# First tree of a Winograd factorization-machine kernel: W11 in two halves, P1 ahead of P5, the fifth linear product in another PSUM tile

## The chip, the cores and the metric

The kernel runs on one core of a Trainium2 chip. Its time is the device time of one execution in microseconds; the figure for the kernel before is the median of three runs, 1403.03 us (1402.93 to 1405.4).

## The reference

A layer of a factorization machine on a batch of 1024 rows, all in float32:

```python
# x (1024, 512), weight (64, 512, 512), lin_w (512, 512), lin_b (512,)
out_lin = x @ lin_w.T + lin_b
xv = einsum('bf,efm->bem', x, weight)
zp = einsum('bf,efm->bem', square(x), square(weight))
return out_lin + 0.5 * sum(square(xv) - zp, axis=1)
```

Nearly all the work is `xv`: a product of 1024x512 by 512x32768, whose result is squared and summed over the 64 embeddings.

## The kernel before, in words

**Tiling.** The 32768 columns are cut into 16 groups of 32 outputs by 64 embeddings. In each group the product goes by two levels of the Strassen-Winograd scheme, seven products in place of eight at each level. The outer level has seven "trees" (`tree(s, g, i, order)`, i from 1 to 7); the first group runs them in the order `ORDER_0 = (1, 2, 6, 7, 5, 4, 3)`. Inside a tree there are seven products `P1` to `P7`; each is two `matmul` calls (two blocks of 128 batch rows, 512 columns each), which the profile shows as four MATMUL records of 128x512 each. The operands of X, seven outer ones with seven inner ones each, live in `x_all` and are made once, at the start, by ScalarE's copies and VectorE's sums (DVE in the profile).

**One tree.** For i = 1 the right-hand matrix is the quadrant W11, in the tile `w11` of shape [128, 2, 2, 512]: the first index of two is the column half c, the second the row half k. So `b11, b21` lie in half c = 0 and `b12, b22` in half c = 1. Four differences come first: `t1 = b12 - b11`, `t2 = b22 - t1`, `t3 = b22 - b12`, `t4 = b21 - t2`. P1 takes b11, P2 takes b21, P3 takes b22, P4 to P7 take t4, t1, t2, t3. In the first tree t1 and t2 are made by VectorE, t3 and t4 by GpSimd (POOL).

**PSUM.** A product writes one of four tiles `b1`, `b3`, `b2_0`, `b2_1`, each of 128x1024 float32. P5 goes to `b3`, ScalarE (ACT) copies it to `p5`, P3 is added to `b3`, ScalarE copies that to `p53`. P1 goes to `b1`, ScalarE copies it to the tree's `b2`, and only then may P2 be added to `b1` and P6 to `b2`. After P6 VectorE adds `b2 + p53` into `oa1`, and then P7 may be added to `b2`; after P7 it adds `b2 + p5` into `oa3`, and then P4 may be added.

**Order.** Nothing is ordered by hand except TensorE's (PE's) products: a product of the tree with place s gets the key `7*s + PLACE[p]`, and for the first tree `7*s + PLACE_0[p]`, and PE takes the keys in rising order. Products of neighbouring trees thus alternate. For the other engines, `Plan.order()` plays the plan through with estimated costs and gives every engine a fixed list, the operation that is needed earliest first among those that its model holds ready. On the chip each engine runs its list in order, with semaphores for the waits. So a change of keys or of an estimated landing can reorder the lists of all engines.

**The start.** Before the trees come four products of the linear layer's own Strassen-Winograd scheme (`lin_product`: 1, 2, 4, 5; keys -1000 to -997), while x and the linear weights still arrive. Their transfers are issued by hand at the head of the two DMA queues (`load_x`, `load_lw`: nine and two on SP's queue), and `landing(name, at)` tells the planner when each is expected. Then `load(g, q)` issues the weight quadrants on SP's queue, in the first group in the order W11, W21, W12, W22, each of 1 MB. After its PSUM result a linear product is copied out by two ScalarE operations with bias (`lin_copy`), each of one half of the tile; the fifth one writes `outer7`, which lies in `w22b`.

ScalarE also squares every quadrant for `zp` (`w_squares`: `wsq<-w`, two per quadrant). In ScalarE's list these stand between the copies of PSUM.

The beginning of PE's list before, in the numbering of the products (the prime marks the second tree, i = 2, on W21): linear 1, 2, 4, 5, then P5 (b3), P1 (b1), P3 (b3), P6 (b2), P5' (b3), P2 (b1), P3' (b3), P7 (b2), P1' (b1). ScalarE's list there: two bias copies of linear product 5, `p5<-b3`, `b2<-b1`, first squares of W12, `p53<-b3`, second squares of W12.

Of the kernel before, what the change touches and what calls it, by code (L numbers as in the profile page):

```python
# [23 lines left out]
SLOT = {1: 0, 7: 1, 2: 2, 4: 3, 5: 4, 6: 5, 3: 6}  # L24

PLACE = {5: -6, 3: -2, 1: 0, 6: 3, 2: 4, 7: 6, 4: 9}
PLACE_0 = {**PLACE, 5: -6, 1: -3, 3: -2, 6: -1}
PE, DVE, ACT, POOL, SP = "PE", "DVE", "ACT", "POOL", "SP"
NONE = ""

# [172 lines left out]
def kernel(  # L203
# [39 lines left out]
    nc = tc.nc  # L243
    NG, NQ, _, NCB, KH, N = weight.shape
# [20 lines left out]
    buf = {}  # L265
# [44 lines left out]
    def two_input(engine, o, a, b, sub, size=1024):  # L310

        costs = {DVE: 0.08 + 1.06 * size / 1024, POOL: 0.14 + 2.19 * size / 1024}

        def emit(e):
            f = engines[e].tensor_sub if sub else engines[e].tensor_add
            f(o, a, b)  # L316

        return {engine: costs[engine]}, emit

    def whole(o, a, b, psum=False):  # L320

        costs, emit = two_input(DVE if psum else POOL, buf[o], buf[a], buf[b], False)
        plan.add(costs, emit, (a, b), (o,))
# [21 lines left out]
    def dma(o, i, reads, writes, move=1.75, on=(SP,)):  # L345
        plan.add(dict.fromkeys(on, 0.45), lambda e: queues[e].dma_start(o, i), reads, writes,
                 land=2.0, move=move)
# [4 lines left out]
    def landing(name, at):  # L352
        plan.add({SP: 0.0}, None, (), (name,), land=at - 2 * plan.HOP)

    def load_x(h, k, lo, hi, at):

        n, r = f"oa{2 * h + k // KH}", k % KH
        nc.sync.dma_start(buf[n][:, r, lo * Q:hi * Q], x_src[:, k, h * H + lo * Q:h * H + hi * Q])
        for u in range(lo, hi):
            landing((n, r, u), at)  # L360
# [20 lines left out]
    load_lw(nc.sync, [2, 3], 1, 9.2)  # L381
    for at, k in enumerate((2, 3, 0, 1)):
        load_x(1, k, 0, 2, 10.0 + 0.8 * at)
    nc.scalar.dma_start(bias[:], lin_b)
    landing("bias", 9.5)
    nc.scalar.preload_act_table(AF.Square)
# [62 lines left out]
    def lin_product(p, bank, first, key, last=None, by_k=False):  # L449

        (a, a_names), (b, b_names) = lhs[p], rhs[p]
        for at, key in enumerate((key, last or key + 0.2) + (key + 0.4, key + 0.6) * by_k):
            if by_k:
                k, u = divmod(at, 2)
                steps = [(k, c, slice(u * Q, (u + 1) * Q)) for c in range(2)]
                names = a_names[at:at + 1] + b_names[k:k + 1]
                tiles = both_halves(bank)
            else:
                steps = [(k, at, slice(0, H)) for k in range(KH)]
                names = a_names + b_names  # L460
                tiles = ((bank, at),)

            def emit(_, steps=steps):
                for k, c, rows in steps:
                    nc.tensor.matmul(  # L465
                        buf[bank][:, c, rows], b[:, k, ts(c, P)], a[:, k, rows],
                        start=first and k == 0 and rows.start == 0, stop=k == KH - 1,
                        skip_group_check=True,
                    )

            plan.add({PE: PAIR / (1 + by_k)}, emit, names + tiles, tiles, key=key)

    def both_halves(bank):
        return (bank, 0), (bank, 1)
# [52 lines left out]
    def lin_store(n, h, c):  # L527
        dma(lin_dram[:, ts(c, 2), ts(h, H)], buf[n], (n,), (("lind", h, c),))
# [10 lines left out]
    def lin_copy(n, bank, c, sign):  # L539

        for u in range(2):
            plan.add(
                {ACT: 0.56},
                lambda _, u=u: nc.scalar.activation(
                    buf[n][:, u, :], buf[bank][:, u, :], AF.Identity,
                    bias=bias[:, 2 * c + u:2 * c + u + 1], scale=sign,
                ),
                ((bank, u), "bias"), ((n, u),),
            )
        used(n, (n, 0), (n, 1))  # L550
# [6 lines left out]
    def used(*names):  # L557

        plan.add({NONE: 0.0}, None, (), names)
# [7 lines left out]
    lin_product(4, "b2_0", True, -998)  # L567
    lin_copy("c_2", "b2_0", 0, 1.0)
    lin_store("c_2", 1, 0)
    lin_product(5, "b1", True, -997)  # L570
    flat = buf["w22b"].rearrange("p c k n -> p (c k) n")
    buf["outer7"], buf["negative"] = flat[:, 0::3], flat[:, 1:3]
    used("outer7", ("lt", 1), ("lt", 4))
    lin_copy("outer7", "b1", 1, -1.0)
    lin_store("outer7", 1, 1)
    lin_store("outer7", 0, 1)
    used("quads", *(("ob0", r, c) for r in range(KH) for c in range(2)), ("ob1", 0, 0), ("ob1", 1, 0))
# [19 lines left out]
    def w(g, q):  # L597
        return q + "ab"[g % 2] if q == "w22" else q

    def load(g, q):  # L600
        n = w(g, QUAD[q])
        dma(buf[n], weight[g, q], (), (n,), 3.5)

    def load_more(n, src, reads=(), move=5.5, view=lambda ap: ap):
# [45 lines left out]
    def tree(s, g, i, order):  # L650
        r = w(g, RHS[i])
        b11, b21, b12, b22 = (buf[r][:, c, k, :] for c in range(NCB) for k in range(KH))
        t = {k: t_ring[k]() for k in range(1, 5)}
        for k, a, b, reads in (
            (1, b12, b11, (r,)),
            (2, b22, buf[t[1]], (r, t[1])),
            (3, b22, b12, (r,)),
            (4, b21, buf[t[2]], (r, t[2])),
        ):
            engine = POOL if s or k > 2 else DVE  # L660
            costs, emit = two_input(engine, buf[t[k]], a, b, True, 512)
            plan.add(costs, emit, reads, (t[k],), both=engine == DVE)
        rhs = {
            1: (b11, r), 2: (b21, r), 3: (b22, r), 4: (buf[t[4]], t[4]),
            5: (buf[t[1]], t[1]), 6: (buf[t[2]], t[2]), 7: (buf[t[3]], t[3]),
        }

        def product(p, b, first):
            op, name = rhs[p]

            def emit(_):
                for j in range(G):
                    nc.tensor.matmul(  # L673
                        buf[b][:, j, :], buf[f"X{i}"][:, SLOT[p], ts(j, P)], op,
                        start=first, stop=True, skip_group_check=True,
                    )

            plan.add({PE: PAIR}, emit, (name, f"{'Y' if p == 7 else 'X'}{i}", b), (b,),
                     key=7 * s + (PLACE if s else PLACE_0)[p])

        def copy(o, b):
            act(buf[o], buf[b], None, (b,), (o,))

        def target(pos):
            if i == 2 and order.index(2) < order.index(6):
                return c_ring()
            return f"{TARGET[i]}{pos}"

        def early(pos):

            return pos == 3 and i in ADDEND_FROM and (
                order.index(i) - order.index(ADDEND_FROM[i]) > 1
            )

        def outer_psum(b, pos):

            if i == 1:
                copy(f"oa{pos}", b)
            elif i == 5:
                o = c_ring()  # L700
                whole(o, f"oa{pos}", b, psum=True)
                whole(f"ob{pos}", f"ob{pos}", b, psum=True)
                finish(g, i, o, pos)
            else:
                o = target(pos)
                whole(o, b, f"{ADDEND[i]}{pos}", psum=True)
                if i in (2, 4, 3):
                    finish(g, i, o, pos)

        def outer_sbuf(b, p, pos):  # L710

            if i == 1:
                whole(f"oa{pos}", b, p, psum=True)
            elif i == 5:
                o = c_ring()
                whole(p, b, p, psum=True)
                whole(o, f"oa{pos}", p)
                whole(f"ob{pos}", f"ob{pos}", p)
                finish(g, i, o, pos)
            else:  # L720
                a, o = f"{ADDEND[i]}{pos}", target(pos)
                if early(pos):
                    whole(o, b, p, psum=True)
                else:
                    z = p if o == a else o
                    whole(z, b, p, psum=True)
                    whole(o, z, a)
                if i in (2, 4, 3):
                    finish(g, i, o, pos)

        b2, p5, p53 = b2_ring(), p5_ring(), p53_ring()
        product(5, "b3", True)
        if early(3):
            whole(p5, "b3", f"{ADDEND[i]}3", psum=True)
        else:
            copy(p5, "b3")
        product(3, "b3", False)
        copy(p53, "b3")
        product(1, "b1", True)
        copy(b2, "b1")  # L740
        product(6, b2, False)
        outer_sbuf(b2, p53, 1)
        product(2, "b1", False)
        outer_psum("b1", 0)
        product(7, b2, False)
        outer_sbuf(b2, p5, 3)
        product(4, b2, False)
        outer_psum(b2, 2)
# [184 lines left out]
    for g in range(NG - 1):  # L933
        group(g, {} if g else {2: lin_tree})
        b, names = turn(g, 3)
        m, c = (g * MG) % P, g * MG // P
# [295 lines left out]
```

## Time and profile before

| what | value |
|---|---|
| time, median of three runs | 1403.03 us |
| the profiled execution's own time | 1403.01 us |
| its span (first to last instruction) | 1401.2 us |
| PE busy | 1395.3 us (100%), 3314 records, granted clock 1.00 |
| VectorE, ScalarE, GpSimd busy | 1099.9, 714.9, 1053.3 us |
| landing of W11, W21, W12, W22 of the first group | 17.0, 19.5, 22.0, 24.4 us |
| first product of the first tree starts | 19.26 us |

Times in the trace count from the start of the span. The profiled execution is 1.8 us longer than its span, and 0.02 us from the median. A MATMUL record of 128x512 lasts 592 ns but the next one starts 429 ns after it, so a gap between records only shows in "idle before" when it is longer than the overlap; start times tell more. The landings are the issue times of the transfers plus the time to landing that the view of line L346 gives for each.

### The profile page before, as it was taken

The page shows a single profiled execution, that of the slowest core. Times are in us where ns is not written, and L with a number is a line of the kernel's source. Part 1 is how long each engine was busy: PE and PEld are TensorE (multiplying, and loading weights), DVE is VectorE, ACT ScalarE, POOL GpSimd, SP SyncE. Part 2 cuts the span into 40 slices and gives each one's busy share as a digit, 9 for nine tenths or more (in the row PEclk, how much of TensorE's full clock was granted, in tenths as well). Part 3 has the DMA queues.
Part 4 walks back from the last instruction along what each step waited for, and adds up shares of the span by engine and source line. Part 5 has one row for each costly group of instructions (what it writes and reads, how often), then busy time and mean ns, then how long its engine had stood idle before and what let it go on. Part 6 is the DMA issues. An engine that isn't in the chain of part 4 may idle for free.

```text
span 1401.2 us, 10709 instructions
## 1 busy us (share of the span) xinstructions
PE 1395.3 (100%) x3314; PEld 629.8 (45%) x3314; DVE 1099.9 (78%) x987; ACT 714.9 (51%) x756; POOL 1053.3 (75%) x750
## 2 busy tenths in 40 slices
PE   9999999999999999999999999999999999999998
PEld 4544444444444444444444444444444444444454
DVE  7998696877959788696877959678696877959676
ACT  4555473545736456373544636355373544636444
POOL 4796776958778586786958678686786958678994
PEclk9999999999999999999999999999999999999999
DMA  7495574827749285582817538183572817538363
GB/s 270 94 221 162 138 180 121 226 74 180 205 121 232 90 196 164 135 221 82 225 51 180 153 99 206 49 196 120 132 178 84 222 53 180 154 97 207 101 165 113
DMA packets 55815, 212.90 MB, mean 152 GB/s; under 512 B 21520, under 2 KB 23056, under 8 KB 33872
## 3 DMA queue, kind: packets, MB, share of 16 engines
q0 software_dynamic: 13136, 84.81, 31.5%
q1 hardware_dynamic: 40352, 125.12, 25.6%
q10 hardware_dynamic: 2272, 2.30, 0.5%
q8 instruction: 27, 0.44, 0.1%
q14 instruction: 28, 0.23, 0.0%
HBM read 180.75 MB, written 14.02 MB: 139 GB/s over the span
## 4 chain that ended last, share of the span: by engine, by line
PE 96%; DVE 1%; DMA 1%; ACT 0%; issue 0%; SPq 0%; DVEq 0%
PE b L673 93%; PE b L826 2%; PE b L465 1%; DMA c<-xT 1%; PE b L1145 1%; DMA oa<-xT 0%; DVE p L316 0%; DVE c L316 0%; DVE ob L316 0%; DVE w_sum L339 0%; ACT ob L332 0%; DVE oa L316 0%; DVE acc L339 0%; ACT c L332 0%; ACT b L328 0%
## 5 line engine op out<-in xcount | busy, mean ns | idle before, releaser
L673 PE MATMUL b<-t,x_all 128*128 128x512 f32 x1792 | 806.4, 592 | 0.2 <-DVE oa L316 0.2
L673 PEld LDWEIGHTS b<-t,x_all 128*128 128x128 f32 x1792 | 340.2, 190 | 426.1 <-issue 417.3
L673 PE MATMUL b<-w,x_all 128*128 128x512 f32 x768 | 358.1, 592 | 0.0
L316 POOL TENSOR_TENSOR t<-w 128x512 f32<-128x512 f32 x127 | 171.3, 1349 | 148.5 <-PE b L673 78.1
L328 ACT COPY p<-b 128x1024 f32<-128x1024 f32 x165 | 165.6, 1003 | 171.0 <-PE b L673 166.2
L673 PEld LDWEIGHTS b<-w,x_all 128*128 128x128 f32 x768 | 145.9, 190 | 183.7 <-issue 182.5
L316 POOL TENSOR_TENSOR t<-w,t 128x512 f32<-128x512 f32 x127 | 171.8, 1353 | 55.1 <-PE b L673 54.8
L332 ACT ACTIVATE oa<-oa 128x1024 f32<-128x1024 f32 x124 | 129.5, 1057 | 144.2 <-DVE oa L316 144.2
L328 ACT COPY b<-b 128x1024 f32<-128x1024 f32 (+1 forms) x114 | 113.5, 996 | 135.7 <-PE b L673 132.0
L673 PE MATMUL b<-T,x_all 128*128 128x512 f32 x384 | 180.3, 592 | 0.0
L339 DVE TENSOR_REDUCE acc<-oa 128x16 f32<-128x1024 f32 x124 | 148.8, 1211 | 36.7 <-ACT oa L332 36.7
L339 DVE TENSOR_REDUCE w_sum<-wsq 128x16 f32<-128x1024 f32 x128 | 153.6, 1209 | 0.3 <-ACT wsq L332 0.2
L332 ACT ACTIVATE c<-c 128x1024 f32<-128x1024 f32 x77 | 79.6, 1055 | 131.6 <-DVE c L316 88.2
L316 DVE TENSOR_TENSOR oa<-b,p 128x1024 f32<-128x1024 f32 x95 | 115.7, 1218 | 33.7 <-PE b L673 33.5
L316 POOL TENSOR_TENSOR t<-T 128x512 f32<-128x512 f32 x64 | 85.7, 1339 | 53.2 <-issue 31.3
L673 PEld LDWEIGHTS b<-T,x_all 128*128 128x128 f32 x384 | 73.0, 190 | 91.0 <-issue 89.4
L316 DVE TENSOR_TENSOR p<-b,p 128x1024 f32<-128x1024 f32 x79 | 96.4, 1220 | 20.9 <-PE b L673 16.8
L316 DVE TENSOR_TENSOR ob<-b,p 128x1024 f32<-128x1024 f32 x48 | 58.6, 1221 | 64.7 <-PE b L673 64.4
L332 ACT ACTIVATE wsq<-w 128x1024 f32<-128x1024 f32 x96 | 98.3, 1054 | 12.0 <-DMA w<-weight 11.1
L316 POOL TENSOR_TENSOR t<-T,t 128x512 f32<-128x512 f32 x64 | 82.4, 1288 | 20.1 <-PE b L673 20.0
L316 POOL TENSOR_TENSOR c<-oa,p 128x1024 f32<-128x1024 f32 x32 | 84.8, 2651 | 0.0
L316 DVE TENSOR_TENSOR oa<-b,oa 128x1024 f32<-128x1024 f32 x62 | 75.6, 1220 | 9.5 <-PE b L673 9.5
(116 smaller groups left out, 1421.4 us busy)
## 6 DMA issues: line engine op xcount, KB each, us to landing
w<-weight SPq DMA_DIRECT2D x48, 1024.0 KB, 5.4
T<-weight POOLq DMA_DIRECT2D x45, 1024.0 KB, 9.2
T<-weight SPq DMA_DIRECT2D x30, 1024.0 KB, 7.2
w<-weight POOLq DMA_DIRECT2D x16, 1024.0 KB, 11.0
w<-T POOLq DMA_DIRECT2D x16, 1024.0 KB, 6.9
w22a<-weight SPq DMA_DIRECT2D x8, 1024.0 KB, 10.8
w22b<-weight SPq DMA_DIRECT2D x8, 1024.0 KB, 10.9
c<-xT SPq DMA_DIRECT2D x9, 512.0 KB, 6.8
```

Source lines behind the costliest of these rows:

```text
L316: f(o, a, b)
L328: nc.scalar.copy(o, i)
L332: nc.scalar.activation(o, i, func)
L339: lambda _: nc.vector.tensor_reduce(o, i.rearrange("p a (m e) -> p a m e", e=E), axis=AX.X, op=ALU.add),
L465: nc.tensor.matmul(buf[bank][:, c, rows], b[:, k, ts(c, P)], a[:, k, rows], start=first and k == 0 and rows.start == 0, stop=k == KH - 1, ...
L673: nc.tensor.matmul(buf[b][:, j, :], buf[f"X{i}"][:, SLOT[p], ts(j, P)], op, start=first, stop=True, skip_group_check=True,)
L826: nc.tensor.matmul(buf[b][:, u, lo:lo + Q], op[z], buf[f"X{x}"][:, SLOT[p], :], start=first and not lo, stop=True, skip_group_check=True,)
L1145: nc.tensor.matmul(o, ap[:, k, ts(u, P)], in_rows(o, buf[raw[i]][:, k, lo:hi]), start=first and k == 0, stop=k == 1, skip_group_check=True,)
```

## The change

```diff
-PLACE_0 = {**PLACE, 5: -6, 1: -3, 3: -2, 6: -1}
+PLACE_0 = {**PLACE, 1: -6, 5: -5, 2: -4, 3: -3, 6: -2, 7: 3}
...
     for at, k in enumerate((2, 3, 0, 1)):
         load_x(1, k, 0, 2, 10.0 + 0.8 * at)
+    for c in range(NCB):
+        nc.sync.dma_start(buf["w11"][:, c], weight[0, 0, :, c])
+        landing(("w11", c), 14.5 + 1.5 * c)
...
-    lin_product(5, "b1", True, -997)
+    lin_product(5, "b3", True, -997)
...
-    lin_copy("outer7", "b1", 1, -1.0)
+    lin_copy("outer7", "b3", 1, -1.0)
...
     def load(g, q):
         n = w(g, QUAD[q])
+        if not g and not q:
+            return used(n, (n, 0), (n, 1))
         dma(buf[n], weight[g, q], (), (n,), 3.5)
...
+        own = r if s else (r, 0)
         rhs = {
-            1: (b11, r), 2: (b21, r), 3: (b22, r), 4: (buf[t[4]], t[4]),
+            1: (b11, own), 2: (b21, own), 3: (b22, r), 4: (buf[t[4]], t[4]),
```

Three things change. The transfer of W11 in the first group is issued by hand, as two transfers of 512 KB, and in the first tree P1 and P2 wait for the first half alone. The keys of the first tree put P1 first, then P5, P2, P3, P6, and P7 at key 3. The fifth product of the linear layer goes to `b3` in place of `b1`, so that P1 finds `b1` free.

PE's list after the linear products becomes: P1 (b1), P5 (b3), P2 (b1), P3 (b3), P6 (b2), P5' (b3), P7 (b2), P3' (b3), P1' (b1). ScalarE's list there: two bias copies of linear product 5 (now from `b3`), first squares of W12, `b2<-b1`, `p5<-b3`, second squares of W12, `oa0<-b1`, `p53<-b3`. VectorE's first 24 operations keep their order. GpSimd's first operation is t1 of W21, then t3 of W11; before, it was the other way round. SP's queue has one transfer more; the order of the others stays. Number and kinds of all other instructions are unchanged, and the lists differ in single swaps until about a quarter of the run.

## The prediction

> **What bounds the kernel now.** I read the page's busy line first, then the chain, then PE's own waits.
>
> ```profile
> PE 1395.3 (100%) x3314; PEld 629.8 (45%) x3314; DVE 1099.9 (78%) x987; ACT 714.9 (51%) x756; POOL 1053.3 (75%) x750
> ...
> PE 96%; DVE 1%; DMA 1%; ACT 0%; issue 0%; SPq 0%; DVEq 0%
> ```
>
> PE is busy for 1395.3 of 1401.2 us, at a granted clock of 1.00, and the change adds and removes no product. So the time can only change by the idle time of PE. PE's waits over the whole span:
>
> ```profile
> PE b L465 <- DMA oa<-xT: 1.1, 1, 1.1
> PE b L391 <- PEq L1221: 0.8, 1, 0.8
> PE b L673 <- DVE oa L316: 0.2, 1, 0.2
> ```
>
> The first two end at 7.04 us, in the loads of x, ahead of everything that is touched. The third lies at 461 us, where the lists of all engines are the same again. What is left to gain sits at the start of the first tree, below the threshold of that view, and shows in the start times of PE's timeline:
>
> ```profile
> 15.73 3.60 PE L465 MATMUL b<-x_all,w22b 128*128 128x512 f32 x8
> 19.26 1.98 PE L673 MATMUL b<-t,x_all 128*128 128x512 f32 x4
> 21.08 3.17 PE L673 MATMUL b<-w,x_all 128*128 128x512 f32 x7
> ```
>
> In steady state four records (one product) take 1.72 us and eight 3.43 (the chain has such pieces throughout), and a group of four shows 1.88 to the end of its last record. From 15.73 the next product is due at 19.16, but starts at 19.26, 0.10 late, and lasts 1.98 instead of 1.88: the weight load that could not run ahead. Its cause is VectorE's t1, which starts at 17.45 and takes 1.75, to 19.20. So 0.20 us is all that the first tree loses now: a gain of 0.2% (2.8 us, about what a measurement of this kernel can tell from no change) isn't there to be had. It can only lose. Therefore I follow the new lists of PE and ScalarE through the next twelve microseconds. ScalarE's timeline, and the transfer of W12 in the view of line L346 (window 10.52 to 10.9: issued at 10.54, landed 11.4 later, 21.97 us):
>
> ```profile
> 19.36 1.27 ACT L544 ACTIVATE w22b<-b,bias 128x512 f32<-128x512 f32 x2 [2.17 <-PE b L465]
> 21.28 1.01 ACT L328 COPY p<-b 128x1024 f32<-128x1024 f32 x1 [0.65 <-PE b L673]
> 23.05 1.00 ACT L328 COPY b<-b 128x1024 f32<-128x1024 f32 x1 [0.76 <-PE b L673]
> 23.96 1.06 ACT L332 ACTIVATE wsq<-w 128x1024 f32<-128x1024 f32 x1
> ```
>
> ```profile
> L346 SPq DMA_DIRECT2D w<-weight x1: 430/430/430, 10.5 to 10.5; - x1
> ...
> DMA to landing us min/median/max: 11.4/11.4/11.4
> ```
>
> Now the squares of W12 start two microseconds after its landing, behind both copies.
>
> **The change part by part.**
>
> *P1 first, on W11.* W11 as a whole lands at 17.02 (issue 9.59 plus 7.4), so P1 starts at 19.16 when linear product 5 leaves PE, and the two halves are not needed for that. b1 is free: VectorE's sum that read it ended at 13.79 (VectorE's timeline: 12.57 plus 1.22). P5 follows at 20.88 and has t1, done by 19.20 (earlier, if GpSimd no longer works beside it: 512 columns took 0.68 us at 9.69), and b3, whose two bias copies end at 20.63. Gain 0.20.
>
> *The wait that the change adds.* In ScalarE's new list the first squares of W12 stand ahead of `b2<-b1`. ScalarE is free at 20.63 and waits for W12 until 21.97. Squares 22.00 to 23.06; the next operation starts 0.10 before the end, as the rows above do, so the copy of P1's result runs 22.96 to 23.96. P2 adds to b1, is due at 20.88 + 1.72 = 22.60, and starts at 24.00: 1.40 late, plus the 0.10 of an exposed weight load. Loss 1.50. PE has nothing else in its list, since it too goes in order.
>
> *What is queued behind.* `p5<-b3` runs to 24.87, and P3 is due at 24.00 + 1.82 = 25.82: covered by 0.9. P6 at 27.54 has b2 and t2 (20.26 plus 1.75 on VectorE). P5' at 29.26 needs `p53<-b3`: P3's last record ends at 27.70, the copy at 28.72, covered by 0.5. P7 at 30.97 is the tightest: P6's last record ends at 29.42, VectorE's add (free since 27.85, takes 1.21) at 30.65, covered by 0.3. If that add took 1.75, as such operations do beside GpSimd, it would cost 0.2. t3 of W11 now follows t1 of W21 on GpSimd: 19.56 + 1.90 + at most 1.9 gives 23.4, seven microseconds before P7. I take nothing for these.
>
> *Two transfers for one.* One more issue costs SP 0.47 us (9.59, 10.06, 10.54 are the issues now), so W12 is issued at 11.01, W22 at 11.49. The transfers ahead end at 19.49, so the issue is covered by 8 us. What counts is W12's landing. Nearest rows: 1 MB loads land 2.47 apart (17.02, 19.49, 21.97), and the 512 KB stores `lind` behind them 1.28 apart (25.72, 26.99, 28.27, 29.55, each the issue plus its time to landing). Two halves thus take 2.56 at most where the whole takes 2.47, and I take W12 at 22.0. But W11 itself took 4.32 after the last load of x (issued 9.11, landed 3.6 later), 1.85 over the 2.47, and the trace does not say why. Bounds: the halves remove that 1.85 (W12 at 20.1), or each half pays it (W12 at 23.8).
>
> [...]
>
> *The sum.* -0.20 + 1.50 = +1.30 us. From the span 1401.2 that makes 1402.5; from the median (0.02 over the profiled execution) 1403.03 + 1.30 = 1404.3 us.
>
> **The rivals.**
>
> *The wait vanishes.* If W12 lands at 20.1, ScalarE squares 20.53 to 21.59 and copies to 22.5, just before P2 is due. Then only the gain remains: 1403.03 - 0.20 = 1402.8. For it: the unexplained 1.85 us sit exactly on the transfer that is split. Against it: P2's stall shrinks one for one with the landing only, and the bytes ahead of W12 are the same. Partial cases lie between.
>
> *Slower by over 0.2%.* Same place, other sign: both halves pay the 1.85, W12 lands at 23.8, P2 is 3.35 late with its load, and the time is 1403.03 - 0.20 + 3.35 = 1406.2. It decides from a landing of 23.5 on (1.5 late). Against it: the 512 KB rows above. The tight cover of P7 (0.2) would add to it, and of the three runs before one stood 2.4 us over the median, so a median can fall there too.
>
> *The change does not do what it says.* P1 doesn't need the first half early, since the whole lands 2.1 us before PE is free. This is certain rather than a rival, and already in the sum: the halves bring nothing on the path.
>
> **How the numbers follow.** Forecast (W12 within 0.7 us of 22.0: 1403.6 to 1405.0, reaching to 1405.8 with a small extra wait): 0.68. Wait gone or nearly (1402.8 to 1403.6): 0.12. Slower by over 0.2% (above 1405.8): 0.18. Faster by over 0.2%: 0.02, because PE's idle time in the touched stretch is 0.2 us. That makes faster 0.02, same 0.68 + 0.12 = 0.80, slower 0.18. The range goes from 1402.8, the sum without the wait, to 1406.2, the upper bound of the landing.
>
> **What would show it.** In PE's waits after, one new row: b at the product line, ended by ScalarE's b copy, about 1.4 us, at 24.0 us in the timeline. In ScalarE's timeline: squares of w idle before by 1.3 us until a DMA, at 22.0, then b, then p. PE's first product of the tree at 19.16 with `b<-w,x_all`. The chain should run through ScalarE at this place to the DMA of w. All the rest of PE's rows should be shifted by 1.3 us and still whole at 461. The prediction is wrong if W12 lands before 21 or after 23.5 us, if the copy of b1 does not wait for the squares, or if a stall appears after 30 us.

## The result, and the profile after

The changed kernel takes 1405.76 us (median of 20 runs, 1404.6 to 1408.62), the kernel before 1402.68 (median of 20, 1402.18 to 1405.4). The ratio is 1.0023 with a 95% interval of 1.0016 to 1.003: slower by 3.1 us. The profiled execution took 1406.77, its span is 1405.0, 3.78 over the span before. PE's busy line on the page, and PE's waits over the whole span:

```profile
PE 1397.2 (99%) x3314; PEld 630.3 (45%) x3314; DVE 1093.8 (78%) x987; ACT 714.1 (51%) x756; POOL 1049.6 (75%) x750
```

```profile
PE b L679 <- ACT b L328: 2.2, 1, 2.2
PE b L394 <- PEq L1227: 0.8, 1, 0.8
PE b L468 <- DVE x_all L316: 0.3, 1, 0.3
```

The first row is new, at the line of the products and ended by ScalarE's `b` copy, as forecast. Before, there was no wait of that kind; but it is 2.2 us and not 1.4, and PE is busy for 1.9 us more although it does the same 3314 records. ScalarE's timeline of the changed kernel gives the cause, and the view of line L346 (window 10.2 to 10.3) the landing of W12:

```profile
19.20 1.26 ACT L547 ACTIVATE w22b<-b,bias 128x512 f32<-128x512 f32 x2 [2.76 <-PE b L468]
22.77 1.06 ACT L332 ACTIVATE wsq<-w 128x1024 f32<-128x1024 f32 x1 [2.30 <-DMA w<-weight]
23.73 1.01 ACT L328 COPY b<-b 128x1024 f32<-128x1024 f32 x1
24.67 1.00 ACT L328 COPY p<-b 128x1024 f32<-128x1024 f32 x1
```

```profile
L346 SPq DMA_DIRECT2D w<-weight x1: 458/458/458, 10.2 to 10.2; - x1
...
  ACT wsq L332: 2.3, 1
...
DMA to landing us min/median/max: 12.5/12.5/12.5
```

W12 was issued at 10.24 and landed at 22.74. ScalarE stood idle for 2.30 us in front of the squares, and the copy of P1 came after them. PE's timeline at this place, and its windows with the granted clock (columns: window, its length, busy time of PE, PEld, DVE, ACT, POOL with counts, PEclk, DMA share, GB/s):

```profile
20.71 1.88 PE L679 MATMUL b<-t,x_all 128*128 128x512 f32 x4
24.79 5.34 PE L679 MATMUL b<-w,x_all 128*128 128x512 f32 x8 [2.19 <-ACT b L328]
```

```profile
22.59:24.70 2.11, 0.01 (x1) 0.00 (x0) 2.11 (x2) 1.93 (x3) 2.11 (x2) 1.00 1.02 406
24.70:28.10 3.40, 3.31 (x4) 1.51 (x5) 0.89 (x1) 1.93 (x3) 3.40 (x4) 0.50 0.95 367
28.10:31.00 2.90, 2.90 (x8) 1.32 (x7) 0.00 (x0) 1.85 (x2) 2.90 (x5) 1.00 0.15 59
```

P2, due at 20.71 + 1.72 = 22.43, starts at 24.79, 2.36 late. And then eight records take 5.34 us instead of 3.60: for 3.4 us after the wait the granted clock is 0.50. That is the extra busy time. This is a second price of the same wait, and I had not counted it.

It is not paid in every run. The record has a mean granted clock for each of the 20 runs. One fall of 3.4 us to 0.50 takes 0.0012 off the mean of a run (an estimate: half of 3.4 us, of 1405 us), so a run at 1.000 had none. Twelve runs are at 1.000, with a median of 1405.6; four are at 0.998 like the profiled one, from 1406.77 to 1407.56; four at 0.999 can be either. The two runs that make the median, 1405.70 and 1405.83, are at 1.000. So the fall belongs to the profiled execution and to some others, but 2.9 of the 3.1 us are there without it.

The last piece is at the very end. The waits of SP's queue in the last microseconds, before and after:

```profile
SPq L1228 <- DMA out<-T: 1.4, 3, 0.5
```

```profile
SPq L1234 <- DMA out<-T: 1.8, 1, 1.8
```

The program ends with a row of waits on the eight DMA semaphores, one after another. Before, three of them end one by one as the last stores land, and in the trace the last store updates the semaphore that the row asks for last. Now it updates the first of the eight: a single wait of 1.8 us stands for the last store, and the other semaphores are asked for only after it, some 0.06 us each. From PE's last record to the end of the span it is 3.89 us before and 4.40 after.

The sum for the two profiled executions: the first tree starts at 19.00 instead of 19.26 (-0.26, of which 0.10 is the end of the wait for t1 and the rest the start of the run: loads that landed earlier, less 0.59 that linear product 5 lost waiting for x, the third of the rows above with its weight load), P2's wait +2.36, the clock +1.73 (the eight records' excess), the exposed weight load behind t1 -0.10, the wait at 461 us gone -0.46, the tail +0.51. That makes 3.78, the difference of the spans. It is a sum for these two executions; the medians lie 3.1 apart.

### The profile page after: what moved, and what is told of

Its sections match the earlier page's. It is cut to its first block, busy times and chain, and to the rows that moved or that the text cites. A ratio compares the mean times of both kernels' runs of the same rounds, so it can differ in the third digit from the quotient of the medians.

```text
span 1405.0 us, 10718 instructions
## 1 busy us (share of the span) xinstructions
PE 1397.2 (99%) x3314; PEld 630.3 (45%) x3314; DVE 1093.8 (78%) x987; ACT 714.1 (51%) x756; POOL 1049.6 (75%) x750
## 4 chain that ended last, share of the span: by engine, by line
PE 98%; DMA 1%; SPq 0%; issue 0%; DVE 0%; ACT 0%; ACTq 0%; DVEq 0%
PE b L679 96%; PE b L832 2%; DMA w<-weight 1%; PE b L1151 1%; DMA ob<-lin_wT 0%; SPq L358 0%; ACT b L328 0%; ACTq L365 0%; SPq L385 0%; DVE T L1130 0%; DVEq L1234 0%; DVE T L1163 0%; SPq L346 0%; ACT wsq L332 0%; ACTq L328 0%
## 5 line engine op out<-in xcount | busy, mean ns | idle before, releaser
L332 ACT ACTIVATE wsq<-w 128x1024 f32<-128x1024 f32 x96 | 98.1, 1052 | 23.2 <-DVE w_sum L339 12.6
```

The lines of the kernel that those rows point to most:

```text
L332: nc.scalar.activation(o, i, func)
```

## The experiments

The theory: the planner no longer has W11 on its model of the DMA wire, since a transfer issued by hand does not advance it; so it holds W12 to land 3.5 us earlier than it does, finds ScalarE free at that time, and puts the squares of W12 ahead of the copies of PSUM. The rivals: the two halves are to blame, or the new order of the products.

**The planner's wire corrected.** The whole change, and one number:

```diff
-        done, late, nxt, wire = [], 0.0, 0, 9.0
+        done, late, nxt, wire = [], 0.0, 0, 12.5
```

> The whole change, but the planner's model of the DMA wire starts at 12.5 us instead of 9.0, so that the hand-issued W11 counts in it as the planned one did; the copies of PSUM then stand ahead of the squares of W12 in ScalarE's list again, and nothing else of the change is undone. Theory (the loss is ScalarE's wait for W12 ahead of the copy of P1, and what the clock does after it): no wait of PE at P2, granted clock 1.00, 0.2 us under the kernel before, ratio 0.9998. Rival one (the two half transfers are to blame): W12 still lands near 22.7 and the time stays near 1405.8, ratio 1.002. Rival two (the new order of the products is to blame): also near 1.002.

Measured: 1404.09 us against 1402.48, ratio 1.0014 (1.0005 to 1.0023). In ScalarE's timeline the copy now stands first and the wait of P2 is gone:

```profile
20.97 1.00 ACT L328 COPY b<-b 128x1024 f32<-128x1024 f32 x1 [0.49 <-ACT w22b L547]
22.65 1.01 ACT L328 COPY p<-b 128x1024 f32<-128x1024 f32 x1 [0.68 <-PE b L679]
23.56 1.06 ACT L332 ACTIVATE wsq<-w 128x1024 f32<-128x1024 f32 x1
```

So the planner's wire is the cause of the list, shown by one number, although both halves and the new order of the products are still in; W12 landed at 22.58, as late as rival one says, and no longer held PE up. The time alone would not settle it, since its interval reaches the 1.002 of the rivals. And it did not come back to 0.9998: the theory as I had written it was short of something. The trace shows what: the tail is 4.40 here too; PE has three small waits, by its start times 0.34 at 29.6 us (P7), 0.31 at 90 and 0.18 at 101; and the execution lies 2.1 us over its span instead of 1.8. Against the second trace of the kernel before (further below) that is 0.52 + 0.83 + 0.32, less 0.40 at the head of the tree, which starts at 19.01 instead of 19.31 and without the exposed weight load: 1.27, and the two executions differ by 1.29 (1403.86 and 1402.57). The medians differ by 1.6. Why 0.3 more lie outside the span, here and in the next but one, stays open.

The wait at P7 is the one I had called tight. VectorE's timeline of this version:

```profile
26.87 1.50 DVE L316 TENSOR_TENSOR x_all<-x_all 128x256 f32<-128x256 f32 x1
28.29 1.21 DVE L316 TENSOR_TENSOR oa<-b,p 128x1024 f32<-128x1024 f32 x1
```

P6's last record had ended at 27.76, but VectorE only gets to the add at 28.29, ends at 29.50, and P7 starts at 29.56 instead of 29.32. In the changed kernel P2's wait covers this.

**W11 whole, through the plan.** New keys and the other PSUM tile, without the halves:

```diff
-    for c in range(NCB):
-        nc.sync.dma_start(buf["w11"][:, c], weight[0, 0, :, c])
-        landing(("w11", c), 14.5 + 1.5 * c)
...
-        if not g and not q:
-            return used(n, (n, 0), (n, 1))
...
-        own = r if s else (r, 0)
+        own = r
```

> New keys and the other PSUM tile, but W11 whole and issued through the plan as before. Theory: the planner has W11 on its wire again, ScalarE's list has the copies first, no wait, ratio 0.9998. Rival one (halves): no halves, so 0.9998 as well. Rival two (order of the products): near 1.002.

Measured: 1403.08 against 1402.48, ratio 1.0004 (0.9995 to 1.0013): no difference that can be told, though not the gain either. The new order of the products is not the loss. Its trace has the wait at P7 (0.16 with the weight load) and 0.7 at 117 to 120 us, no wait at P2, tail 3.88. The versions with two and three spare copies (below) have the same 0.7 us at this place and the kernel before has not, so it comes with this version's lists; together with P7 it outweighs the gain at the head of the tree.

**The halves alone.** The old keys and the old PSUM tile:

```diff
-PLACE_0 = {**PLACE, 1: -6, 5: -5, 2: -4, 3: -3, 6: -2, 7: 3}
+PLACE_0 = {**PLACE, 5: -6, 1: -3, 3: -2, 6: -1}
...
-    lin_product(5, "b3", True, -997)
+    lin_product(5, "b1", True, -997)
```

> Two hand-issued halves alone, with the old keys and the old PSUM tile; ScalarE's list has the first squares of W12 ahead of the copy to p5. Theory: P3, due at 22.7, waits for W12 (22.0 to 22.7) plus squares plus copy, 1.3 to 2.1 us, and 1.7 more in runs where the clock falls to half afterwards: ratio 1.001 to 1.003. Rival one (halves slow down the loads): about the same, 1.002. Rival two (order of the products): no loss, 1.000.

Measured: 1406.33 us, ratio 1.0026 (1.0017 to 1.0036), as much as the whole change. So the loss does not need the new order. W11 is issued by hand here too, so this run does not part the halves from the planner's mistake. Now P3 waits for the copy to `p5`, behind the same squares:

```profile
PE b L679 <- ACT p L328: 1.5, 1, 1.5
```

In this profiled execution the clock stayed whole, and it took 1403.97; the other eight lie between 1406.2 and 1406.9. I had expected a fall of the clock in such runs, but five of the eight have a mean granted clock of 1.000, so they had none. The profiled execution had early loads (its first tree starts at 18.03 us, in the eleven other traces at 18.60 to 20.87), which would be a part of the difference. The rest is open, since the other eight have no trace.

**One transfer by hand.**

```diff
-    for c in range(NCB):
-        nc.sync.dma_start(buf["w11"][:, c], weight[0, 0, :, c])
+    nc.sync.dma_start(buf["w11"], weight[0, 0])
+    for c in range(NCB):
         landing(("w11", c), 14.5 + 1.5 * c)
```

> The whole change, but W11 issued by hand as one transfer of 1 MB; ScalarE's list as in the change. Theory: W12 lands near 22.0 instead of 22.7, P2 waits about 1.5 us instead of 2.4; ratio 1.001 if the clock stays whole, 1.002 if it falls. Rival one (halves): no loss, 0.9998. Rival two (order of the products): 1.002 as the change.

Measured: 1403.96 us, ratio 1.001 (1.0001 to 1.0019), with the clock whole. P2 is 1.22 late here, W12 landed at 22.34, and the tail is 3.87. So the planner's mistake costs without any halves. Over all traces of this study the time from the issue of the last load of x to the landing of W12 is 12.6 to 13.9 us, mean 13.07, in the eight with W11 whole, and 13.4 to 14.8, mean 14.07, in the four with halves: 1.0 us later on average, in ranges that overlap. This run's 13.87 is the top of the eight, and it alone of them issues W11 by hand; so whether the halves cost the whole 1.0 us, or issuing by hand a part of it, one trace does not tell. In all twelve traces W12 lands 4.93 to 5.02 us after the last of W11: what is lost is lost ahead of W11's landing.

**The price of a wait by itself.** On the version with W11 whole and planned, spare copies stand on ScalarE ahead of the copy of P1; `k` is 2, 3 and 4:

```diff
-        copy(b2, "b1")
+        if s:
+            copy(b2, "b1")
+        else:
+            def late_copy(_):
+                for _ in range(k):
+                    nc.scalar.copy(buf["wsq_0"], buf["ob2"])
+                nc.scalar.copy(buf[b2], buf["b1"])
+
+            plan.add({ACT: 1.04}, late_copy, ("b1",), (b2,))
```

> The version with W11 whole and planned (new keys, other PSUM tile), and two spare copies of 1024 columns on ScalarE ahead of the copy of P1: the copy ends about 0.9 us after P2 is due. Theory (a wait of PE costs its length, and 1.7 us more when the clock falls to half after it, which needs a longer wait): P2 about 0.9 late, clock whole, 1 us over the version without them, ratio 1.0011. Rival (the wait is made up later, or costs its length alone): 1.0011 too.

> As before with three spare copies: P2 about 1.8 late. Theory: part of the runs with the clock at half for 3.4 us: 1.9 to 3.6 us over the version without them, ratio 1.0017 to 1.003, spread over two groups. Rival (length alone): 1.0017 in all runs.

> As before with four spare copies: P2 about 2.7 late. Theory: clock at half in nearly all runs, 2.8 plus 1.7, 4.5 us over the version without them, ratio 1.0036, granted clock 0.5 for 3.4 us after the wait in the profile. Rival (length alone): 2.8 over, 1.0024.

Measured: 1404.05, 1405.17 and 1407.62 us, ratios 1.001 (1.0001 to 1.0019), 1.002 (1.0011 to 1.0029) and 1.0037 (1.0024 to 1.0051). P2 is late by 1.01, 2.09 and 3.16 by its start times. PE's waits at the copy of P1, with two, three and four spare copies:

```profile
PE b L674 <- ACT b L747: 0.8, 1, 0.8
```

```profile
PE b L674 <- ACT b L747: 1.9, 1, 1.9
```

```profile
PE b L674 <- ACT b L747: 3.0, 1, 3.0
```

Against 1403.08 without spare copies the time grows by 1.0, 2.1 and 4.5: the wait's own length twice, and 1.4 more the third time. Windows of the versions with three and with four copies:

```profile
22.68:24.61 1.93, 0.01 (x2) 0.00 (x1) 1.93 (x2) 1.93 (x3) 1.93 (x2) 1.00 1.01 395
24.61:28.40 3.79, 3.79 (x9) 1.81 (x10) 3.79 (x4) 2.90 (x4) 3.79 (x5) 1.00 0.89 344
```

```profile
22.38:25.00 2.62, 0.00 (x1) 0.00 (x0) 2.62 (x3) 2.59 (x3) 2.62 (x3) 1.00 1.02 400
25.00:28.40 3.40, 3.02 (x4) 1.47 (x5) 2.98 (x3) 2.22 (x3) 3.40 (x4) 0.50 0.87 336
```

With 1.93 us idle the clock stays at 1.00, with 3.0 (PE's waits) it goes to 0.50 for 3.4. For three copies I expected two groups of runs; there is one, with a single run at 1406.57 beside it, whose clock is 1.000. None of the three waits was made up later.

**One spare store.** The kernel before, with one store of 2 KB in mid-run:

```diff
+    spare = dram.tile([P, M // P], F32, tag="spare", name="spare")
...
+        if at == 2000:
+            nc.sync.dma_start(spare, bias[:])
```

> The kernel before with one spare store of 2 KB on SP's queue in mid-run and nothing else. Theory (one transfer more turns the ring of eight DMA semaphores by one, so that the last store's semaphore is no longer the one that the closing waits ask for last): the time from PE's last record to the end of the span goes from 3.89 to 4.40 us, ratio 1.0003 to 1.0004. Rival (the longer tail of the change came from its order or its halves): 3.89, ratio 1.0000.

Measured: 1402.89 against 1402.44, ratio 1.0005 (0.9996 to 1.0014), so the interval does not part it from no change. The trace does: 4.41 us from PE's last record to the end, and SP's closing waits are those of the changed kernel:

```profile
SPq L1231 <- DMA out<-T: 1.9, 1, 1.9
```

The five traces with one transfer more have 4.39 to 4.41, the seven without 3.87 to 3.89. In the trace with the spare store the last store again updates the first of the eight semaphores, and without it the last. The tail thus goes with the number of transfers, not with the order of the products or the halves.

**Both kernels once more.**

> The changed kernel once more, for a second trace. [...] Time 1404.5 with the clock whole, 1406.5 with it fallen.

> The kernel before once more, for a second trace: P3 not late, tail 3.89, waits of 0.2 at the first product of the tree and 0.5 at 461 us or so, which come and go with the loads; time 1402.4. It tells whether the three small waits of 0.2 to 0.3 us that the version with the longer wire shows (at 30, 90 and 101 us) are of that version or of the run.

The kernel before took 1402.57 us; its trace has the wait of t1 (0.25) and none at 461, so that one comes and goes, and none at 30, 90 and 101, so those belong to the other version. The changed kernel took 1406.33 with its clock whole, where I had expected 1404.5. Its waits:

```profile
PE b L679 <- ACT b L328: 1.5, 1, 1.5
PE b L468 <- DVE x_all L316: 1.4, 1, 1.4
```

P2 is 1.77 late with its weight load. The 1.4 is linear product 5, 1.68 late by its start times with its weight load, which I had not expected. It waits for VectorE's x sum and that for the last load of x, landed at 15.93 instead of 12.70: in the trace's packets W11's run beside those of x (in the first trace of the change from 11.0 us on, while x landed at 14.06; in the first of the kernel before from 11.9 on, with x at 12.70). W12 landed at 23.93 here. From issue to landing the last load of x took 4.3 to 6.8 us in the five traces that issue W11 by hand and 3.6 to 5.4 in the seven others. So it changes from run to run, and whether the change has a part in it is not shown.

## Why the prediction was right or wrong, point by point

- *The mechanism and its place: right.* P2 waits for the copy of P1, which stands behind the squares of W12. The number that makes the list so, the planner's wire, was found only afterwards; correcting it took the wait away.
- *The size of the wait, 1.50: too small.* It was 2.36, 1.77 with its weight load in the second trace. The step that failed is W12's landing, taken at 22.0 from the spacing of the stores. It was 22.74, and 23.93 in the second trace, which is past the 23.5 that I had named as a sign of being wrong; there the tree itself started 1.9 us later, so that P2 was less late. With halves W12 lands 1.0 us later on average, inside the bounds I had given (20.1 to 23.8) but not at the value I took from the nearer row.
- *The loads of x: left out.* I took what lies ahead of the tree as untouched. Linear product 5 lost 0.59 and 1.68 us waiting for x in the two traces of the change and nothing in those of the kernel before; other versions have it or not, and whether it is the change's stays open.
- *The split as free at the landing: not borne out.* I took two halves to land as the whole does (2.56 us at most for 2.47), from the 1.28 us between the 512 KB stores. Measured, W12 lands 1.0 us later with the split, on average (14.07 us after the issue of the last load of x, against 13.07). Once under way the transfers do land 1.25 apart for 512 KB (16.53 and 17.78); the loss is ahead of W11's landing, since behind it W12 follows after 4.93 to 5.02 us in all twelve traces.
- *No price for the clock: missing.* I priced the wait at its length and an exposed weight load. When the clock falls, the same wait costs 1.4 (four copies) to 1.7 us more (the changed kernel's profiled execution); in twelve of the 20 runs it did not fall.
- *One transfer more is free: wrong.* I followed its issue on SP (covered, as said) and not its turn in the ring of semaphores, 0.5 us at the end of the run.
- *P7's cover of 0.3: held in the changed kernel*, and gave way as soon as P2 no longer waited.
- *The sum, 1404.3, and the chances: low.* 1.30 + 1.0 for W12 + 0.5 for the tail is 2.8, near the 2.9 of the twelve runs without a fall of the clock. The difference of 3.1 is over twice the forecast one; the time is 1.5 over the forecast and not 1.8, because the kernel before measured 1402.68 in the end and not 1403.03. That 1405.76 lies in the range is partly luck: I had worked out the upper end, 1406.2, from W12 at 23.8 alone, and the tail and the loads of x, which I had left out, took up a part of that room. It lies 0.04 under the 1405.8 at which the rival "slower by over 0.2%" was to begin, and the ratio of 1.0023 is over 0.2% with an interval that takes 0.2% in, so the runs don't part that rival, which I gave 0.18, from the forecast. Its mechanism (W12 late) was a good half of the matter; its point of decision, a landing of 23.5, was too late, since other costs stood beside it.

## What to carry to other kernels

When a transfer is taken out of a planner's hands, look at what its model of the queue then believes of the transfers behind it: the list of another engine can change, and an in-order engine that waits for data holds up everything behind it (here ScalarE's 2.30 us for W12 stood ahead of the copy of P1, and P2 started 2.36 us late). Price a wait of a saturated TensorE at its length only while it is short (here waits of 0.8 and 1.9 us cost 1.0 and 2.1, one of 3.0 cost 4.5); look at the granted clock just after it. And count the transfers: where a program closes with waits on a ring of semaphores, one more can move the end (here from 3.89 to 4.41 us after PE's last record).

## What the runs showed of the hardware that was not expected

- The granted clock fell to 0.50 for 3.4 us after PE had been idle for 2.1 us (the changed kernel, 22.59 to 24.70 us) and 2.6 us (four copies, 22.38 to 25.00) ahead of the fall, in waits of 2.2 and 3.0 us. It did not after waits of 1.9 (three copies), 1.5 (the halves alone, and the changed kernel once more), 1.1 (one transfer by hand) and 0.8 us (two copies). In the trace's clock record the falls, at 24.70 and 25.01 us, lie 20.48 us after the record first shows the clock whole in the same run (4.22 and 4.53): six times the 3.41 us that the changed kernel's fall lasts. Whether the length of the gap alone decides, these runs don't show.
- Where one 1 MB load (packets of 8 KB in the trace) was split in two (packets of 4 KB), right behind loads with packets of 2 KB, W12 behind it landed 1.0 us later on average (14.07 against 13.07 us after the issue of the last load of x), four traces against eight, in ranges that overlap. Why is open.
- The wait of the closing semaphores went with which of them the last store has: 3.89 us from PE's last record to the end when it is the one asked for last (the kernel before), 4.40 and 4.41 when it is the first (the changed kernel, one spare store).
